# A graph network layer pair on one core: by-edge weights kept in PSUM, window sums and constants sharing two banks

## The chip, the cores and the metric

The kernel runs on one core of one Trainium2 chip. The metric is the device time of one execution in microseconds (us). A profile is one execution, recorded by the hardware; its span runs from the first to the last instruction of the program. Engines are named as in the profile: PE (TensorE, matmuls; PEld its weight loads), DVE (VectorE), ACT (ScalarE), POOL (GpSimd, which issues the gathers), SP (SyncE, which issues the plain DMAs).

## The reference

A graph has 6250 nodes of 128 features and 100000 edges, sorted by their destination. Two layers run one after the other, each with a residual sum and a layer norm over the features.

```python
# layer 0: mean of messages
m = relu(nfeat[src] @ W_ne[:128] + (efeat @ W_edge) @ W_ne[128:] + b_ne)
neigh = segment_sum(m, dst) / max(count(dst), 1)
x = layernorm(x + neigh + x @ W_self + b_self)

# layer 1: attention over the edges (and a loop on each node), 4 heads of 32
xl = x @ w_l + b_l;  xr = x @ w_r + b_r
e = leaky_relu(xl[src] + xr[dst], 0.2)
logits = einsum('ehc,hc->eh', e, att)
ex = exp(logits - segment_max(logits, dst)[dst])
alpha = ex / segment_sum(ex, dst)[dst]
out = segment_sum(xl[src] * alpha, dst) + bias
out = (out - out.mean()) / (out.std() + 1e-5) * ln_w + ln_b
x = layernorm(x + out)
```

## The kernel before

The edges are cut into 196 groups of 512 (four tiles of 128). Because they are sorted, the destinations of a group lie in a window of 96 node rows. The function `near` holds both edge stages. Each stage gathers the source rows of its groups from DRAM by indirect DMAs on POOL (`gather`, L339, four to a group, 128 rows each).

**First edge stage** (`e0`, steps of the loop at L559). Messages are formed on PE, DVE and ACT, and the sums over a window are matmuls with a one-hot matrix (`onehot`, L393 to L397: 1 where the edge's destination is that row of the window). The change touches only where `onehot` finds its constant row 0 to 95, `iota_q`.

**Second edge stage** (`e1`, L593 to L912). The order on each engine is the order in which the lines of the step loop (L887) are written; nothing is rescheduled. Step `s` does, in this order:

- `gather1(s + 4)`: the four gathers on POOL. A group's rows stay in one of 30 buffers until `values` has read them.
- `store_sums` and the planned `out_load`, `m_load`, `m_logits`.
- `copy_both(s - 1)` on ACT, `both(s)` on PE: `z` becomes xl[src] + xr[dst], transposed, in PSUM (`pz`).
- `leaky(s - 1)` on DVE, `logits(s - 2)` on PE, `onehot_t(s + 1)` on ACT.
- for each group due in this step: `sums(u)` (four matmuls into `pa`, then `old` on DVE takes the window of the group before, scaled, and one more small matmul adds its last row), `keep_sums(u)` (ACT copies `pa` to SBUF).
- for each group due in the next step: `values_w(u)` (ACT copies weight and maximum by edge into `v`), `values(u)` (DVE multiplies the gathered rows by the weights), `onehot(u)`.
- the rest of the plan: steps of the softmax chain, and outputs of finished blocks (`out_weights`, `output` with `ready`, which multiplies by ln_w).

**The softmax chain.** Twelve groups (nine and seven in the last two) make a macro; its logits lie in one tile with a row for each head and group. `M_STEPS` lists ten functions, one to a step, that find the running maxima by scans, the maximum carried over from one group to the next, and the weights: `m_logits`, `m_forward`, `m_back`, `m_ends`, `m_groups`, `m_before`, `m_maxima`, `m_weights`, `m_left`, `m_ready`. The last three turn weights and maxima from rows to edges: transposes into the PSUM tile `pw` (`by_edge`), and ACT copies of it into the SBUF tile `wm` (`keep_by_edge`). A macro's first group is due `len(M_STEPS) + 1` steps after the chain begins; from 30 steps before the last group on, two groups may fall due in one step. `output` of a block comes five steps after its last group is stored.

**PSUM.** There are eight banks. Before, the second stage has two for `pz`, two for `plg` (logits), two for `pa`, one for `pw` (also used by `m_ends` and `m_before`), and one, `rows_q`, for constants that DVE alone reads: `iota_q` and `lnw_q` (ln_w). `rows_q` lives through both stages.

Of the kernel before, what the change touches and what calls it, by code (L numbers as in the profile page):

```python
# [9 lines left out]
F32 = mybir.dt.float32  # L10
F32R = mybir.dt.float32r
# [6 lines left out]
P = 128  # L18
N = 6250
E = 100000  # L20
D = 128
# [53 lines left out]
def gnn_resnorm(  # L75
# [268 lines left out]
    def near():  # L344
        ctx = ExitStack()
        with ctx:
# [13 lines left out]
            kps = ctx.enter_context(tc.tile_pool(name="nearp", bufs=1, space=PSUM))  # L360
            rows_q = kps.tile([P, W + D], F32, name="rows_q")
            iota_q, lnw_q = rows_q[:, 0:W], rows_q[:, W:]
            nc.vector.tensor_copy(iota_q, iota_w)
            nc.vector.tensor_copy(lnw_q, lnw_b)
# [28 lines left out]
            def onehot(pool, g, dtype):  # L393

                a = pool.tile([P, G, W], dtype, name="a")
                nc.vector.tensor_tensor(a, over(iota_q, G), spread(dl[:, g * G:(g + 1) * G], W), op=OP.is_equal)  # L396
                return a  # L397
# [13 lines left out]
            with tc.tile_pool(name="e0", bufs=3) as pool, tc.tile_pool(name="e0p", bufs=2, space=PSUM) as ps, \  # L411
# [7 lines left out]
                pt = ps1.tile([P, 2, G // 2, P], F32, name="pt")  # L419
                EF, XG, FT, PX, XS, PH, OH, PA, WIN = {}, {}, {}, {}, {}, {}, {}, {}, {}  # L420
# [138 lines left out]
                for s in range(-2, max(steps) + 1):  # L559
# [22 lines left out]
                    if group(2) is not None:  # L582
                        OH[s - 2] = onehot(pool, s - 2, F32R)
# [9 lines left out]
            with tc.tile_pool(name="e1", bufs=3) as pool, tc.tile_pool(name="e1m", bufs=2) as mp, \  # L593
# [104 lines left out]
                def m_ends(m):  # L698
                    m.pe = ps1.tile([P, S], F32, name="pw")
                    for i in range(2):  # L700
                        nc.tensor.transpose(m.pe[0:1, i * P:i * P + m.R], m.ends[:, i:i + 1], ident[0:m.R, 0:m.R])

                def m_groups(m):
# [4 lines left out]
                    for i in range(2):  # L708
                        nc.vector.tensor_copy(seq[:, i, :, 1:],
                                              m.pe[0:1, i * P:i * P + m.R].rearrange("p (h g) -> p h g", h=H))  # L710
# [9 lines left out]
                def m_before(m):  # L720
                    m.pv = ps1.tile([P, S], F32, name="pw")
                    nc.tensor.matmul(m.pv[0:m.R, 0:1], m.prev_r.rearrange("p h g -> p (h g)"), ones[0:1, 0:1],
                                     start=True, stop=True)

                def m_maxima(m):
                    R = m.R
                    prev = mp.tile([R, 1], F32, name="prev")
                    nc.vector.tensor_copy(prev, m.pv[0:R, 0:1])
# [13 lines left out]
                def by_edge(m, i, t):  # L742
                    m.pw = ps1.tile([P, S], F32, name="pw")
                    for j in range(G):
                        nc.tensor.transpose(m.pw[:, j * m.R:(j + 1) * m.R], t[:, j * P:(j + 1) * P],
                                            ident[0:m.R, 0:m.R])

                def keep_by_edge(m, i):
                    nc.scalar.copy(m.wm[:, :, i].rearrange("p j h g -> p j (h g)"),
                                   m.pw[:, 0:G * m.R].rearrange("p (j r) -> p j r", j=G))  # L750

                def m_weights(m):
                    R = m.R
                    m.wm = mp.tile([P, G, 2, H, m.mg], F32, name="wm")
# [5 lines left out]
                    nc.tensor.matmul(m.pw[:, G * R:(G + 1) * R], ones[0:R, :], dg, start=True, stop=True)  # L760
# [12 lines left out]

# [113 lines left out]
                for s in range(stop + 1):  # L887
# [20 lines left out]
                    for u in due.get(s + 1, ()):  # L908
                        values_w(u)
                        values(u)  # L910
                        OH[u] = onehot(pool, u, F32)
# [333 lines left out]
```

## Time and profile before

The median of three runs is 2222.46 us (2222.4 to 2223.11). The profiled execution took 2217.53 us, with a span of 2215.8 us and a mean granted PE clock of 0.837.

The span falls into these stretches. Each number is busy time in us; PEclk is the granted clock as a share of full speed.

| stretch, us | length | PE | DVE | ACT | POOL | PEclk |
|---|---|---|---|---|---|---|
| 45 to 1016: first edge stage | 971 | 633.0 | 589.6 | 207.1 | 734.8 | 0.78 |
| 1016 to 1052: between the stages | 36 | 14.5 | 26.0 | 3.3 | 0.1 | 0.59 |
| 1052 to 1190: second stage, no group due yet | 138 | 101.6 | 27.7 | 54.2 | 105.1 | 0.72 |
| 1190 to 1880: one group a step | 690 | 580.3 | 396.8 | 321.5 | 526.3 | 0.99 |
| 1880 to 2057: also two groups or none | 177 | 154.8 | 127.2 | 82.1 | 135.5 | 0.89 |
| 2057 to 2156: after the last gather | 99 | 70.8 | 74.3 | 18.8 | 0.0 | 0.64 |
| 2156 to 2216: last outputs and norm | 60 | 1.1 | 43.1 | 23.1 | 0.0 | 0.50 |

A row of the timeline gives start and length in us, the engine, the line, the operation, and what it writes and reads; in square brackets stands the idle time before it and what ended it. POOL counts as busy while an indirect DMA is being prepared; between two of them there are 0.30 us in which it waits for nothing that the profile shows. In the groups, `xN` is the number of instructions, then busy us and mean ns of one, then the idle time before them.

### The profile page before, as it was taken

The numbers are of one execution on the slowest core, as the hardware profiler recorded it, in microseconds if no ns is written. First come the engines' busy times: TensorE is split into PE (matmuls) and PEld (weight loads), VectorE is DVE, ScalarE is ACT, GpSimd is POOL, SyncE is SP. The second block draws the span as 40 slices with busy tenths as digits, with TensorE's granted clock in tenths as the row PEclk, the third lists the DMA queues.
The fourth block names the chain that finished last, engine by engine and source line by source line (L and its number), as shares of the span: only waits on it lengthen the run. The fifth ranks groups of instructions, "written<-read, shape, count | busy, mean of one in ns | idle before, by whom it ended". The sixth has DMA issues, their size and how long they took to land.

```text
span 2215.8 us, 26713 instructions
## 1 busy us (share of the span) xinstructions
PE 1569.5 (71%) x6565; PEld 878.3 (40%) x6565; DVE 1304.2 (59%) x3709; ACT 713.4 (32%) x1723; POOL 1511.0 (68%) x1575
## 2 busy tenths in 40 slices
PE   3786566566556566665678888888888888889760
PEld 2664444444344444443123333333333333434440
DVE  5664455556556666777123555555565666677777
ACT  1331211121112222221344444444444444444214
POOL 3777777777777777772777777777777777777100
PEclk9997767777777778776778999999999999989755
DMA  4654344434444444432433444444444444443102
GB/s 122 155 116 90 88 95 95 98 89 103 100 102 96 103 105 108 106 89 59 134 103 101 114 112 113 114 115 112 116 116 113 113 111 113 116 119 100 29 23 62
DMA packets 292630, 225.34 MB, mean 102 GB/s; under 512 B 143289, under 2 KB 247591, under 8 KB 292466
## 3 DMA queue, kind: packets, MB, share of 16 engines
q1 hardware_dynamic: 240624, 120.21, 20.5%
q0 software_dynamic: 50048, 102.60, 19.6%
q8 instruction: 56, 0.92, 0.2%
q10 hardware_dynamic: 1794, 0.73, 0.2%
q14 instruction: 108, 0.88, 0.1%
HBM read 189.85 MB, written 33.52 MB: 101 GB/s over the span
## 4 chain that ended last, share of the span: by engine, by line
DMA 21%; POOL 21%; PE 19%; DVE 19%; issue 17%; ACT 2%; DVEq 0%; SPq 0%; ACTq 0%; POOLq 0%
POOL xg L339 21%; DMA xg<-xw_t,src_i 11%; DMA xg<-xl_t,src_i 9%; PE pa L790 5%; PE plg L661 3%; PE pz L635 3%; DVE a L396 3%; DVE msg L480 2%; PE pz L633 2%; PE pa L796 2%; DVE v L781 1%; PE ph L462 1%; DVE win L494 1%; DVE ln_st L211 1%; DVE old L794 1%
## 5 line engine op out<-in xcount | busy, mean ns | idle before, releaser
L339 POOL DMA_INDIRECT xg<-xl_t,src_i x782 | 767.0, 981 | 274.4 <-issue 173.2
L339 POOL DMA_INDIRECT xg<-xw_t,src_i x738 | 697.3, 945 | 224.9 <-issue 186.5
L642 DVE SCALAR_TENSOR_TENSOR z<-z,pz 128x512 f32<-128x512 f32 x196 | 134.6, 686 | 381.0 <-ACT z L639 375.3
L471 DVE TENSOR_TENSOR ph<-ph,xg 128x512 f32<-128x512 f32 x185 | 129.5, 700 | 336.1 <-DMA xg<-xw_t,src_i 302.3
L476 ACT ACTIVATE msg<-ph 128x512 fp32r<-128x512 f32 x196 | 117.3, 599 | 549.1 <-DVE ph L471 513.8
L633 PE MATMUL pz<-ident,xg 128*128 128x128 f32 x784 | 189.3, 317 | 148.0 <-DMA xg<-xl_t,src_i 131.7
L462 PE MATMUL ph<-wc,fT 128*128 128x256 f32 x784 | 286.5, 502 | 0.0
L489 PE MATMUL pa<-win,sel 96*1 96x129 f32 x390 | 90.2, 321 | 248.8 <-DVE win L494 247.5
L790 PEld LDWEIGHTS pa<-v,a 128*96 128x96 f32 x1568 | 200.9, 175 | 157.7 <-issue 111.8
L790 PE MATMUL pa<-v,a 128*96 128x136 f32 x1568 | 248.2, 305 | 8.6 <-DVE a L396 5.2
L661 PE MATMUL plg<-z,attw 128*48 128x512 f32 (+2 forms) x392 | 229.1, 669 | 0.0
L635 PE MATMUL pz<-ds,xr 96*128 96x512 f32 x392 | 219.4, 643 | 0.0
L396 DVE TENSOR_TENSOR a<-rows_q,dl 128x384 fp32r<-128x384 f32 (+1 forms) x392 | 214.7, 548 | 0.0
L801 ACT COPY win<-pa 96x136 f32<-96x136 f32 x196 | 52.5, 268 | 480.9 <-PE pa L796 448.9
L462 PEld LDWEIGHTS ph<-wc,fT 128*128 128x128 f32 x784 | 182.2, 251 | 59.1 <-issue 31.4
L633 PEld LDWEIGHTS pz<-ident,xg 128*128 128x128 f32 x784 | 95.6, 145 | 263.8 <-DMA xg<-xl_t,src_i 186.8
L487 PE MATMUL pa<-msg,a 128*96 128x258 f32 x784 | 180.5, 364 | 0.0
L626 ACT ACTIVATE ds<-ds,nb 96x512 f32<-96x512 f32 x196 | 142.1, 725 | 8.7 <-DMA xr<-xr_t 8.6
L627 ACT ACTIVATE ds<-ds,ones 96x512 f32<-96x512 f32 x196 | 141.5, 722 | 6.4
L480 DVE SCALAR_TENSOR_TENSOR msg<-ph,msg 128x512 fp32r<-128x512 f32 x196 | 135.6, 692 | 3.4 <-ACT msg L476 3.4
L487 PEld LDWEIGHTS pa<-msg,a 128*96 128x96 f32 x784 | 134.6, 212 | 1.0 <-PE pa L487 0.4
L639 ACT COPY z<-pz 128x512 f32<-128x512 f32 x196 | 113.5, 579 | 66.5 <-PE pz L635 66.4
(204 smaller groups left out, 1776.1 us busy)
## 6 DMA issues: line engine op xcount, KB each, us to landing
ds<-dpad SPq DMA_DIRECT2D x196, 192.0 KB
ef<-in_edge_attr_dram SPq DMA_DIRECT2D x48, 512.0 KB
xg<-xl_t,src_i POOLq DMA_INDIRECT x782
xg<-xw_t,src_i POOLq DMA_INDIRECT x738
out_t<-win SPq DMA_DIRECT2D x196, 51.0 KB
sum_t<-win SPq DMA_DIRECT2D x196, 48.4 KB
xr<-xr_t SPq DMA_DIRECT2D x196, 48.0 KB
s<-out_t SPq DMA_DIRECT2D x47, 68.0 KB
```

Source lines behind the costliest of these rows:

```text
L339: nc.gpsimd.indirect_dma_start(out=to, out_offset=None, in_=table[0:min(table.shape[0], NP), :], in_offset=bass.IndirectOffsetOnAxis(ap=in ...
L396: nc.vector.tensor_tensor(a, over(iota_q, G), spread(dl[:, g * G:(g + 1) * G], W), op=OP.is_equal)
L462: nc.tensor.matmul(ph[:, 2 * i:2 * i + 2, :], fT[:, i, :], wc, start=i == 0 or g >= RAW, stop=g >= RAW, skip_group_check=g < RAW)
L480: nc.vector.scalar_tensor_tensor(msg[:, :, 1, 0:D], PH.pop(g), 0.0, msg[:, :, 0, 0:D].bitcast(F32), op0=OP.max, op1=OP.subtract)
L487: nc.tensor.matmul(pa, a[:, j, :], msgs[g % 3][:, j], start=j == 0, stop=j == G - 1)
L626: nc.scalar.activation(DS[g], DS[g], AF.Abs, bias=nb[0:W, g:g + 1])
L627: nc.scalar.activation(DS[g], DS[g], AF.Relu, bias=ones[0:W, 0:1], scale=-1.0)
L633: nc.tensor.matmul(pz[:, j * P:(j + 1) * P], XG[g][:, j, :], ident, is_transpose=True, start=j == 0, stop=False, skip_group_check=True)
L635: nc.tensor.matmul(pz, XR.pop(g), DS.pop(g), start=False, stop=True, skip_group_check=True)
L642: nc.vector.scalar_tensor_tensor(Z[g], Z[g], SLOPE, PZ.pop(g), op0=OP.mult, op1=OP.max)
L661: nc.tensor.matmul(m.plg, attw[m.mg][:, m.mg - i:m.mg - i + m.R], Z.pop(g), start=i == 0, stop=i == m.mg - 1)
L790: nc.tensor.matmul(pa, a[:, j, :], v[:, j].rearrange("p h c -> p (h c)"), start=j == 0, stop=j == G - 1)
```

## The change

Four things are done in the second edge stage, and one in the first:

1. The tiles `pw` and `wm` become one PSUM tile of a full bank, in two buffers: the transposes write weights and maxima by edge straight to the layout that `values_w` and `values` read, and these read PSUM. `keep_by_edge` and the step `m_ready` go; the chain has nine steps, so a macro's groups are due one step earlier.
2. The window sums `pa` no longer come from a pool of two: even groups use the bank `pb[0]`, odd ones `pb[1]`.
3. The constants `iota_q` and `lnw_q` stand beside the sums in `pb[0]`. The bank `rows_q` goes.
4. The small results of `m_ends` and `m_before` stand beside the sums in `pb[1]` (`few`), not in `pw`.
5. The first stage gets an `iota_q` of its own, handed to `onehot`.

```diff
-            kps = ctx.enter_context(tc.tile_pool(name="nearp", bufs=1, space=PSUM))
-            rows_q = kps.tile([P, W + D], F32, name="rows_q")
-            iota_q, lnw_q = rows_q[:, 0:W], rows_q[:, W:]
-            nc.vector.tensor_copy(iota_q, iota_w)
-            nc.vector.tensor_copy(lnw_q, lnw_b)
...
-            def onehot(pool, g, dtype):
+            def onehot(pool, g, dtype, iota_q):
...
+                iota_q = ps1.tile([P, W], F32, name="iota_q")
+                nc.vector.tensor_copy(iota_q, iota_w)
...
+                pb = [ps1.tile([P, 4 * P], F32, name=f"pb{i}") for i in range(2)]
+                HS = H * HV
+                iota_q, lnw_q, few = pb[0][:, HS:HS + W], pb[0][:, HS + W:HS + W + D], pb[1][:, HS:HS + 2 * P]
+                nc.vector.tensor_copy(iota_q, iota_w)
+                nc.vector.tensor_copy(lnw_q, lnw_b)
...
                 def m_ends(m):
-                    m.pe = ps1.tile([P, S], F32, name="pw")
                     for i in range(2):
-                        nc.tensor.transpose(m.pe[0:1, i * P:i * P + m.R], m.ends[:, i:i + 1], ident[0:m.R, 0:m.R])
+                        nc.tensor.transpose(few[0:1, i * P:i * P + m.R], m.ends[:, i:i + 1], ident[0:m.R, 0:m.R])
...
                 def m_before(m):
-                    m.pv = ps1.tile([P, S], F32, name="pw")
-                    nc.tensor.matmul(m.pv[0:m.R, 0:1], m.prev_r.rearrange("p h g -> p (h g)"), ones[0:1, 0:1],
+                    nc.tensor.matmul(few[0:m.R, 0:1], m.prev_r.rearrange("p h g -> p (h g)"), ones[0:1, 0:1],
                                      start=True, stop=True)
...
                 def by_edge(m, i, t):
-                    m.pw = ps1.tile([P, S], F32, name="pw")
                     for j in range(G):
-                        nc.tensor.transpose(m.pw[:, j * m.R:(j + 1) * m.R], t[:, j * P:(j + 1) * P],
+                        nc.tensor.transpose(m.wm[:, j, i].rearrange("p h g -> p (h g)"), t[:, j * P:(j + 1) * P],
                                             ident[0:m.R, 0:m.R])
-
-                def keep_by_edge(m, i):
-                    nc.scalar.copy(m.wm[:, :, i].rearrange("p j h g -> p j (h g)"),
-                                   m.pw[:, 0:G * m.R].rearrange("p (j r) -> p j r", j=G))
...
                 def m_weights(m):
                     R = m.R
-                    m.wm = mp.tile([P, G, 2, H, m.mg], F32, name="wm")
+
+                    m.pw = ps.tile([P, 4 * P], F32, name="pw")
+                    m.wm = m.pw[:, 0:2 * G * R].rearrange("p (j k h g) -> p j k h g", j=G, k=2, h=H)
...
-                    nc.tensor.matmul(m.pw[:, G * R:(G + 1) * R], ones[0:R, :], dg, start=True, stop=True)
+                    nc.tensor.matmul(m.pw[:, 2 * G * R:(2 * G + 1) * R], ones[0:R, :], dg, start=True, stop=True)
...
                 def m_left(m):
-                    keep_by_edge(m, 0)
                     m.cb = mp.tile([P, H, m.mg], F32, name="cb")
-                    nc.vector.tensor_copy(m.cb, m.pw[:, G * m.R:(G + 1) * m.R].rearrange("p (h g) -> p h g", h=H))
+                    nc.vector.tensor_copy(m.cb, m.pw[:, 2 * G * m.R:(2 * G + 1) * m.R].rearrange("p (h g) -> p h g", h=H))
                     by_edge(m, 1, m.mx)
 
-                def m_ready(m):
-                    keep_by_edge(m, 1)
-
-                M_STEPS = (m_logits, m_forward, m_back, m_ends, m_groups, m_before, m_maxima, m_weights, m_left,
-                           m_ready)
+                M_STEPS = (m_logits, m_forward, m_back, m_ends, m_groups, m_before, m_maxima, m_weights, m_left)
...
-                    pa = PA[u] = ps.tile([W, H * HV], F32, name="pa")
+                    pa = PA[u] = pb[u % 2][0:W, 0:HS]
```

More of the change, by code (lines that the diff above doesn't have):

```diff
@@ L582, in near @@
                     if group(2) is not None:
-                        OH[s - 2] = onehot(pool, s - 2, F32R)
+                        OH[s - 2] = onehot(pool, s - 2, F32R, iota_q)
                     do(window, 4)
@@ L709, in m_groups @@
                         nc.vector.tensor_copy(seq[:, i, :, 1:],
-                                              m.pe[0:1, i * P:i * P + m.R].rearrange("p (h g) -> p h g", h=H))
+                                              few[0:1, i * P:i * P + m.R].rearrange("p (h g) -> p h g", h=H))
                     run = mp.tile([1, H, mg + 1], F32, name="run")
@@ L727, in m_maxima @@
                     prev = mp.tile([R, 1], F32, name="prev")
-                    nc.vector.tensor_copy(prev, m.pv[0:R, 0:1])
+                    nc.vector.tensor_copy(prev, few[0:R, 0:1])
                     fp = mp.tile([R, S], F32, name="fp", bufs=1)
@@ L910, in near @@
                         values(u)
-                        OH[u] = onehot(pool, u, F32)
+                        OH[u] = onehot(pool, u, F32, iota_q)
                     planned(s, but=FIRST)
```

## The prediction

> **What bounds the kernel now.** I read the page's busy table and costliest groups first, then the stretches of the second edge stage, the list of waits, and the timeline in three places: a steady step, a long gather, and the end of the stage.
>
> ```profile
> PE 1569.5 (71%) x6565; PEld 878.3 (40%) x6565; DVE 1304.2 (59%) x3709; ACT 713.4 (32%) x1723; POOL 1511.0 (68%) x1575
> L339 POOL DMA_INDIRECT xg<-xl_t,src_i x782 | 767.0, 981 | 274.4 <-issue 173.2
> L749 ACT COPY wm<-pw 128x192 f32<-128x192 f32 x30 | 9.3, 312 | 1.4 <-PE pw L760 0.9 <-PE pw L745 0.5
> ```
>
> The second edge stage issues 782 gathers on POOL from 1051.9 to 2057.0 us. A gather lasts 0.944 us at the median and the next starts 0.30 us later: 1.249 us, four to a group, 5.0 us a step. POOL never stands idle longer than that 0.3 us there (the largest "issue" wait in the list of waits is 0.3). The other engines wait for gathers: PE loses 131.7 us before pz L633. So up to about 1900 us the stage lasts as long as POOL issues, and what follows the last gather (2057.0 to 2154.9 us, the last group's sums) is a chain through DVE, PE and ACT.
>
> Some gathers are longer. In this row the gather begins 0.04 us after `values` and lasts 1.46 us:
>
> ```profile
> 1178.41 0.68 DVE L781 TENSOR_TENSOR v<-xg,wm 128x512 f32<-128x512 f32 x1
> ...
> 1178.45 1.46 POOL L339 DMA_INDIRECT xg<-xl_t,src_i  x1 [0.30 <-issue]
> ```
>
> I put all 782 gathers beside the DVE rows: where L781 runs 0.14 us after a gather's start, 59 are long, and their excess over 0.944 us sums to 15.7 us. All excess of all gathers is 28.9 us (scans, `pen`, `mx` and `old` make the rest).
>
> The end of the stage, one step with two groups (DVE, PE, ACT; each line is start, length, engine, line, tiles):
>
> ```profile
> 2135.55 0.29 DVE L794 TENSOR_TENSOR old<-pa,cb 96x136 f32<-96x136 f32 x1
> ...
> 2135.90 0.61 PE L796 MATMUL pa<-old,sel 96*1 96x136 f32 x2 [2.08 <-DVE old L794]
> ...
> 2136.44 2.13 PE L790 MATMUL pa<-v,a 128*96 128x136 f32 x8
> 2136.55 0.27 ACT L801 COPY win<-pa 96x136 f32<-96x136 f32 x1 [0.67 <-PE pa L796]
> ...
> 2136.85 0.30 DVE L794 TENSOR_TENSOR old<-pa,cb 96x136 f32<-96x136 f32 x1 [1.00 <-ACT win L801]
> 2137.06 0.68 DVE L781 TENSOR_TENSOR v<-xg,wm 128x512 f32<-128x512 f32 x1
> ...
> 2138.50 0.61 PE L796 MATMUL pa<-old,sel 96*1 96x136 f32 x2
> ...
> 2139.14 0.27 ACT L801 COPY win<-pa 96x136 f32<-96x136 f32 x1 [2.33 <-PE pa L796]
> ...
> 2139.31 0.40 ACT L777 COPY v<-wm 128x32 f32<-128x32 f32 x2
> ...
> 2142.19 0.29 DVE L794 TENSOR_TENSOR old<-pa,cb 96x136 f32<-96x136 f32 x1
> ```
>
> The reader is to see the order: `values` for the next groups (2137.06) starts while PE still multiplies this step's second group (2136.44 to 2139.11). It has no need of the ACT copy L777, which comes 2.25 us later. From `old` to the next `old` is 6.64 us.
>
> **The change, part by part.**
>
> *Removed: 34 copies L749 on ACT.* 34 x 0.31 = 10.6 us of an engine that is 32% busy: 0. They end one wait, though (below).
>
> *`values` reads its weights from PSUM.* Its length: L781 is 678 ns with both inputs in SBUF, L642 is 686 with one in PSUM, same size; +0.01 x 196 = 2 us of DVE, hidden under the gathers. With one SBUF input left, the 59 collisions go. The price lies between 0 (its new place in the step lets other rows fall on gathers) and -15.7; I take **-12**, by the rows: L642 and L396, which read PSUM and SBUF, run as often and go with 3 long gathers, 0.3 us. Here a rule speaks against this term. The Trainium skill ("SBUF — State Buffer", section "Who interferes with whom") has DVE instructions with two SBUF inputs contend with a GpSimd instruction that reads SBUF, but infers that descriptor generation needs only the write side, and so that tensor_tensor does not hold it up; by that inference the term would be 0 and the sum 12 us higher. The 1.46 us row shows the hold.
>
> *New waits.* Two engines' accesses to one bank are put in order in this kernel, reads too: `cb` L765 waits 41.4 us for the ACT copy L749 of the same bank in the trace. In the changed program, as built, `values` of each group waits for ACT's `values_w` of that group; every second `onehot` waits for PE's sums in the bank that holds the constants; the sums of an even group wait for DVE's last read of that bank, which is `ready`'s multiplication in a step with an output; `m_ends` and `m_before` wait for ACT's copy of the sums. `values_w` stands on ACT behind `keep_sums`, which waits for the step's last sums. So `values`, and behind it on DVE `onehot`, the planned work X of the step (outputs, scans) and the next step's `leaky` and `old`, start after PE's sums instead of beside them. PE waits for `old`, then POOL for nothing.
>
> Step with one group, full clock. PE alone: 0.59 + 0.86 + 0.97 + 1.10 + 0.37 = 3.9 us (the chain of waits at 2059 us: pz, pz, plg, pa, last sum). The new chain: win and v 0.5, `values` 0.60, `onehot` 0.47 (starts in the timeline), X, `leaky` 0.61, `old` and its wait 0.29, last sum 0.35: 2.8 + X. An output is X = 2.0, its first half 0.8, scans 1.1 to 1.5, `m_maxima` 2.1: at most some 5 us, against 5.0 to 5.07 for POOL. Before about 1880 us it is hidden by the gathers; without that cover each output would cost about 1 us, some 30 in all.
>
> Step with two groups beside gathers (18 steps, from about 1905 us). PE: 5.3 us (last sums 2059.34 to 2064.65). New chain: 1.8 (both sums) + 0.45 + 2.14 + X + 0.60 + 0.33 = 5.3 + X, so X comes on top. X by the plan written in the kernel, a number for each step that has any: 0.8 + 2.0 + 1.0 + 2.0 + 3.5 = 9.3 us in the first run of such steps, 1.1 + 1.1 + 1.5 = 3.7 in the second, 1.1 + 1.5 + 0.9 = 3.5 in the third. In the steps without groups that lie between, PE has under 3 us of work and half of the first 13.0 can be caught up; the last can't. 6.5 + 3.5 = **+10**; bounds 3.5 and 16.5. Six waits of `m_ends`/`m_before` for the ACT copy, 0.4 each: **+2**.
>
> Steps after the last gather, at half clock as above (7 passages from a step with two groups to the next). New: `old` to last sum 0.35, both sums to their end 3.21 (2135.90 to 2139.11), ACT 0.45, `values` and `onehot` twice 2.14, X 2.98: 9.13 against 6.64, **+2.5** each. Where the first of the pair is even (180 to 188) and the step has an output, its eight matmuls (2.06) wait for X as well instead of running under it: another 2.06 + 0.07 - 0.35 = 1.8. Three passages at 4.3 and four at 2.5: +23. One step fewer in the chain saves the wait for the last copy: 2130.43 + 0.25 less the end of the transposes at 2130.39, and some issue, 0.3 to 1: together **+22**. At full clock the pair ends in 1.81 and the eight in 1.10: 3 x 1.9 + 4 x 1.1 = 10, the lower bound; the upper is 30, as some waits of `m_weights` on DVE (1.2 each) fall there too.
>
> *Constants.* One copy more (L363 0.26, L364 0.28 us), and they now stand at the start of the stages, where POOL waits 36.3 us for stores: 0; uncovered 0.8. `few` takes the place of pw's bank: no cost but the two waits counted. First stage: same instructions.
>
> Sum: -12 + 10 + 2 + 22 = **+22 us**. The profiled execution has a span of 2215.8 and a time of 2217.53; the median of the runs is 2222.46, 4.9 above it. 2222.5 + 22 = **2244**.
>
> The Trainium skill ("PSUM — Partial Sum Buffer", the section on bank collisions) wants PSUM guarded by bank and quadrant and not by address, reads against reads included, and names different banks as the remedy; this change goes the other way. If only addresses counted, the +34 would fall away and -12 stay.
>
> **The rivals.**
> 1. *The stage leaves POOL before 1880 us.* For: 2.8 + X is near 5 us wherever an output falls, the matmul waits on even groups add 0.3, and the granted clock dips to 0.86 to 0.91 in some 12 us stretches after 1800. Against: single steps without X need 3.9 and catch up. If half of the 30 us shows and the gather gain is lost under it: 2244 + 15 = 2259, or up to 2272.
> 2. *The gathers win.* DVE's work is bunched behind the sums, so all 28.9 us of excess go, and the clock stays full behind the last gather: -28.9 + 4 + 2 + 10 = -13, 2210: faster. It decides where the gathers end earlier by more than the 17 us that the rest then costs. For: POOL bounds 1000 us, the end only 100. Against: scans and `pen` keep two SBUF inputs, and PE's clock fell to 0.5 from 2084 us on, after a shorter wait than the new ones.
> 3. *Both cancel*: 12 to 16 of gain against the 16 of the lower bounds: 2222.
> 4. *It doesn't do what it says*: the waits are in the built program, so that isn't left.
>
> **How the numbers follow.** Forecast 2244 (own range 2228 to 2256) 0.55; rival 1 0.20; rival 2 0.16; rival 3 0.09. A measurement of this kernel tells 0.2%, 4.4 us, from no change (the three runs lie within 0.7). Slower 0.76, with a little of rival 3 lost to either side; same 0.08; faster 0.16. The range leaves out the far parts of rivals 1 and 2: 2216 to 2264.
>
> **What would show it.** Gathers behind `values` back at 0.944 us and the last gather near 2045; `values` directly behind `values_w` in every step; DVE idle before it, released by ACT; PE's sums released by `ready` L336 in steps with an even group; from the last gather to the last sums some 34 us longer (22 later, from a gather 12 earlier). It is wrong if the gathers end as before, if the passages at the end stay at 6.6 us, or if POOL waits for buffers before 1880.

## The result, and the profile after

The changed kernel takes 2291.17 us (median of four runs, 2278.91 to 2296.3), against 2222.43 us for the kernel before in the same measurement: a ratio of 1.0306 (95% interval 1.0279 to 1.0334). The forecast was 2244 with a range up to 2264: the direction is right, the size is not. The profiled execution has a span of 2294.6 us (before 2215.8) and took 2296.3 us; the mean granted PE clock fell from 0.837 to 0.806.

Seven of the experiments' runs (e1 to e4, and e9 to e11) come from two measurements in which the kernel before took 2820 us: the gathers paused there, in the first stage too (in e3, 61 pauses beyond the usual 0.30 us, 222 us in all; none in the profile before). Why is not known. The chip's number does not tell: e9 to e11 stand on record under that of e5 to e8, where the kernel before took 2219.6 us. From those seven runs only rows that do not hang on the gathers are read, and their kernels, or a close form, were run again in another measurement ("elsewhere" below).

From the page of the changed kernel, its busy table and groups (what it writes and reads, count, busy us, mean ns, idle before and what ended it):

```profile
PE 1604.7 (70%) x6565; PEld 905.8 (39%) x6565; DVE 1307.4 (57%) x3710; ACT 699.5 (30%) x1689; POOL 1501.4 (65%) x1575
...
L339 POOL DMA_INDIRECT xg<-xl_t,src_i x782 | 757.1, 968 | 330.1 <-issue 219.0
...
L775 DVE TENSOR_TENSOR v<-xg,pw 128x512 f32<-128x512 f32 x196 | 134.4, 686 | 355.1 <-ACT v L771 355.1
```

The same 6565 matmuls keep PE busy 35 us longer than before (1569.5). The gathers are 9.9 us shorter in sum, but POOL stands idle 56 us more. And `values` (L775) was released 169 times by the ACT copy `values_w` (L771), after 355 us of idle DVE. Before, DVE was not idle in front of it:

```profile
L781 DVE TENSOR_TENSOR v<-xg,wm 128x512 f32<-128x512 f32 x196 | 132.9, 678 | 0.0
```

In the list of waits (engine, line and releaser: us in total, times, longest) three of PE's waits for DVE have grown, for `old`, `cb` (14.6 us before) and `dg` (3.6 us before). Before:

```profile
PE pa L796 <- DVE old L794: 20.6, 13, 3.1
```

After, with a fourth that is new, the sums of an even group behind `ready` (L336):

```profile
PE pb L790 <- DVE old L788: 66.4, 50, 3.3
...
PE pb L784 <- DVE xl L336: 23.9, 10, 4.4
...
PE pw L746 <- DVE cb L763: 21.2, 14, 1.8
PE pw L759 <- DVE dg L755: 21.2, 14, 3.5
```

The list puts three more waits of this fourth kind, 19.9 us in all, on L811, the instruction behind `ready`: PE starts 0.15 us after L336 ends in each of them.

Where the time went is read by groups. I took the start of the ACT copy of the window sums (L795; L801 before) of each group, counted from the stage's first gather, and subtracted the same of the kernel before:

| up to the sums of group | what runs there | lag in us | gained or lost since the row above |
|---|---|---|---|
| 0 | first sums, a chain of nine steps instead of ten | -6.8 | -6.8 |
| 140 | one group a step | +31.8 | +38.6 |
| 175 | two groups or none a step, gathers still running | +52.3 | +20.5 |
| 195 | mostly behind the last gather | +76.1 | +23.8 |

With 1.9 us before the stage and 0.8 behind it this is the 78.8 us between the spans. Half of the loss lies where one group falls due in a step. One trace is one execution: in that of e16, the same kernel again, the three rows are +28.6, +20.5 and +23.9 us, so the first of them varies by 10 us. The stretches of the changed kernel (length; busy us of PE, PEld, DVE, ACT, POOL with counts; granted PE clock; DMA share; GB/s):

```profile
1190.00:1530.00 340.00, 292.86 (x1250) 137.27 (x1250) 178.04 (x432) 149.38 (x348) 258.31 (x269) 0.92 0.42 112
1530.00:1880.00 350.00, 290.31 (x1207) 139.69 (x1205) 201.75 (x583) 146.32 (x346) 256.99 (x266) 0.88 0.40 109
```

Before, the clock was 1.00 and 0.99 in these two stretches, with 1281 and 1292 matmuls instead of 1250 and 1207. PE is as busy as it was, but at a lower clock. From the first sums to those of group 120, 2301 matmuls each: 518.4 us of busy PE in 614.5 us before, 546.0 in 643.9 after. PE's matmuls last 27.6 us longer, and 29.4 us are lost. That the two are near each other does not yet show that one is the other; the experiments below price the clock.

One macro shows how that comes. Its timeline (start, length, engine, line, operation; idle before and its end in brackets), from the sums of one step to the matmul after `cb`:

```profile
1606.60 1.17 PE L784 MATMUL pb<-v,a 128*96 128x136 f32 x8
1607.08 0.68 DVE L737 TENSOR_TENSOR lg<-lg,mx 48x512 f32<-48x512 f32 x1
...
1609.02 0.69 DVE L646 SCALAR_TENSOR_TENSOR z<-z,pz 128x512 f32<-128x512 f32 x1 [1.13 <-ACT z L643]
1609.63 0.29 DVE L788 TENSOR_TENSOR old<-pb,cb 96x136 f32<-96x136 f32 x1
...
1609.97 0.39 PE L790 MATMUL pb<-old,sel 96*1 96x136 f32 x2 [2.20 <-DVE old L788]
...
1610.57 0.19 ACT L771 COPY v<-pw 128x32 f32<-128x32 f32 x1
1610.79 0.69 DVE L775 TENSOR_TENSOR v<-xg,pw 128x512 f32<-128x512 f32 x1 [0.87 <-ACT v L771]
1611.39 0.55 DVE L391 TENSOR_TENSOR a<-pb,dl 128x384 f32<-128x384 f32 x1
1611.86 0.23 DVE L755 TENSOR_SCALAR dg<-ident,sc 48x48 f32<-48x48 f32 x1
...
1612.15 0.66 PE L759 MATMUL pw<-dg,ones 48*128 48x48 f32 x2 [1.41 <-DVE dg L755]
...
1613.64 1.91 PE L639 MATMUL pz<-ds,xr 96*128 96x512 f32 x2
...
1615.48 1.94 PE L665 MATMUL plg<-z,attw 128*48 128x512 f32 x2
...
1621.23 0.45 PE L746 MATMUL pw<-ident,mx 48*128 48x48 f32 x4 [1.75 <-DVE cb L763]
```

DVE starts `values` only behind the ACT copy, which stands behind the sums. So `maxima` (L733 to L739) pushes `leaky` (L646) and `old` back. `leaky` waits another 1.13 us for ACT's copy of `z`, which stands behind the exponentials of `maxima` on ACT. So PE waits 2.20 us for `old`; then `dg` waits on DVE behind `values` and the one-hot, and PE waits 1.41 us in the weights step; then `cb` in the left step, 1.75 us. After the first two waits pz L639 and plg L665 take 1.91 and 1.94 us instead of 1.02 and 1.06. The granted clock of these stretches shows why (start and end; length; busy us of PE with count; granted clock; DMA share; GB/s):

```profile
1611.86:1618.69 6.83, 6.54 (x16) 0.50 0.37 90
...
1622.10:1625.52 3.42, 3.42 (x6) 0.50 0.44 125
```

In the 3.41 us ahead of each, PE was busy 0.77 and 1.66 us at a clock of 1.00.

Steps in which nothing else is planned take 3.9 us, as forecast; the weights and left steps take 8.7 and 7.4 us, and gathers for a step take 5.0. Three of twelve steps are of this long kind, and the others catch up only a part. Up to group 42 the lag still falls back to -5.7 us; from there it grows. (By the plan no output stands beside the first 36 groups, and three or four in twelve from group 96 on.) From 1693.7 us on POOL itself waits for buffers that `values` frees late (17 times; in e16 from 1809 us on).

### The profile page after: what moved, and what is told of

The parts are those of the page before. It is cut to its first block, busy times and chain, and to the rows that moved or that the text cites. A ratio compares the mean times of both kernels' runs of the same rounds, so it can differ in the third digit from the quotient of the medians.

```text
span 2294.6 us, 26567 instructions
## 1 busy us (share of the span) xinstructions
PE 1604.7 (70%) x6565; PEld 905.8 (39%) x6565; DVE 1307.4 (57%) x3710; ACT 699.5 (30%) x1689; POOL 1501.4 (65%) x1575
## 3 DMA queue, kind: packets, MB, share of 16 engines
q1 hardware_dynamic: 240624, 120.21, 19.6%
## 5 line engine op out<-in xcount | busy, mean ns | idle before, releaser
L339 POOL DMA_INDIRECT xg<-xl_t,src_i x782 | 757.1, 968 | 330.1 <-issue 219.0
L775 DVE TENSOR_TENSOR v<-xg,pw 128x512 f32<-128x512 f32 x196 | 134.4, 686 | 355.1 <-ACT v L771 355.1
L784 PEld LDWEIGHTS pb<-v,a 128*96 128x96 f32 x1568 | 211.5, 182 | 226.1 <-issue 152.9
L784 PE MATMUL pb<-v,a 128*96 128x136 f32 x1568 | 258.5, 314 | 58.0 <-DVE xl L336 23.9
L665 PE MATMUL plg<-z,attw 128*48 128x512 f32 (+2 forms) x392 | 246.3, 715 | 0.0
L639 PE MATMUL pz<-ds,xr 96*128 96x512 f32 x392 | 240.3, 699 | 0.0
L646 DVE SCALAR_TENSOR_TENSOR z<-z,pz 128x512 f32<-128x512 f32 x196 | 132.9, 678 | 137.2 <-ACT z L643 124.3
L637 PE MATMUL pz<-ident,xg 128*128 128x128 f32 x784 | 163.3, 322 | 55.7 <-DMA xg<-xl_t,src_i 44.0
L795 ACT COPY win<-pb 96x136 f32<-96x136 f32 x196 | 52.5, 268 | 455.3 <-PE pb L790 441.8
```

The costliest lines, as they stand in the source:

```text
L339: nc.gpsimd.indirect_dma_start(out=to, out_offset=None, in_=table[0:min(table.shape[0], NP), :], in_offset=bass.IndirectOffsetOnAxis(ap=in ...
L637: nc.tensor.matmul(pz[:, j * P:(j + 1) * P], XG[g][:, j, :], ident, is_transpose=True, start=j == 0, stop=False, skip_group_check=True)
L639: nc.tensor.matmul(pz, XR.pop(g), DS.pop(g), start=False, stop=True, skip_group_check=True)
L646: nc.vector.scalar_tensor_tensor(Z[g], Z[g], SLOPE, PZ.pop(g), op0=OP.mult, op1=OP.max)
L665: nc.tensor.matmul(m.plg, attw[m.mg][:, m.mg - i:m.mg - i + m.R], Z.pop(g), start=i == 0, stop=i == m.mg - 1)
L775: nc.vector.tensor_tensor(V[u][:, :, :, 2:], XG.pop(u).rearrange("p j (h c) -> p j h c", h=H), m.wm[:, :, 0, :, u - m.g0].unsqueeze(3).to_ ...
```

## The experiments

Mean length of a step, from one group's copy of the sums to the next, by the planned work behind it (groups 0 to 139, steps with no output; 17 or 24 steps in the first column, 7 in each of the others; us):

| kernel | nothing planned | maxima | weights | left |
|---|---|---|---|---|
| before | 5.11 | 5.06 | 5.11 | 5.26 |
| changed | 3.94 | 6.15 | 8.74 | 7.44 |
| e5, weights copied to SBUF | 4.90 | 5.77 | 5.34 | 5.37 |
| e6, sums in banks of their own | 3.86 | 6.16 | 8.49 | 7.90 |
| e7, values first | 4.84 | 5.04 | 4.72 | 4.84 |
| e8, dg and cb first | 4.31 | 6.57 | 6.35 | 4.23 |
| e12, ACT copy first | 4.77 | 5.79 | 5.91 | 5.37 |
| e16, changed kernel again | 3.97 | 6.27 | 8.37 | 6.98 |
| e17, PE's waits filled | 4.13 | 6.64 | 7.01 | 6.10 |

**Which half of the change (e1 and e5; e2 and e6).** Two kernels that each undo one half. In the first, the weights come from SBUF:

```diff
                     by_edge(m, 1, m.mx)
+                    m.ws = mp.tile([P, G, 2, H, m.mg], F32, name="ws")
+                    nc.scalar.copy(m.ws.rearrange("p j k h g -> p (j k h g)"), m.pw[:, 0:2 * G * m.R])
...
-                    nc.scalar.copy(V[u][:, :, :, 0:2], m.wm[:, :, :, :, u - m.g0].rearrange("p j k h -> p j h k"))
+                    nc.scalar.copy(V[u][:, :, :, 0:2], m.ws[:, :, :, :, u - m.g0].rearrange("p j k h -> p j h k"))
...
-                                            m.wm[:, :, 0, :, u - m.g0].unsqueeze(3).to_broadcast([P, G, H, C]),
+                                            m.ws[:, :, 0, :, u - m.g0].unsqueeze(3).to_broadcast([P, G, H, C]),
```

> The changed kernel, but one ACT copy per macro (128x384) puts weights and maxima into SBUF, and values and values_w read them there; the fixed banks, the constants in them and the nine steps stay. Theory A (the loss comes from values, which waits for ACT's values_w of the same PSUM bank and so for PE's sums, and delays dg and cb behind it): values runs beside the sums again, the weights and left steps fall from 8.7 and 7.4 us to 5 or less, the last gather ends near 2060 us instead of 2104, the time is 2225 to 2245 (the end keeps the waits of the shared sum banks). Theory B (the shared banks of sums and constants cause it: one-hot behind PE's sums, even sums behind the output): little changes, 2270 to 2295.

> The kernel of weights_sbuf once more (weights and maxima copied to SBUF once per macro; fixed banks, constants in them and nine steps stay), since in the runs before the gathers themselves paused on that chip, in the first stage too, and the kernel before took 2821 us. Where the kernel before takes about 2222 us: theory A (values waits for ACT's values_w and so for PE's sums, and delays dg and cb) 2225 to 2245; theory B (shared banks of sums and constants) 2270 to 2295.

In the second, the sums leave the shared banks, and `few` becomes a part of `m.pw`, which is taken from its pool in `m_ends`:

```diff
-                    pa = PA[u] = pb[u % 2][0:W, 0:HS]
+                    pa = PA[u] = ps.tile([W, H * HV], F32, name="pa")
...
-                    ready(pool, b0, n, lnw_q)
+                    ready(pool, b0, n)
...
-                        OH[u] = onehot(pool, u, F32, iota_q)
+                        OH[u] = onehot(pool, u, F32, iota_w)
```

> The changed kernel, but the sums have their own two banks as before, the constants are read from SBUF, and m_ends and m_before use the macro's weight bank; weights and maxima stay in PSUM and the chain has nine steps. Theory A (values behind values_w behind the sums): still slow, 2265 to 2295, weights step over 7 us; some of the end (even sums behind the output, 5 to 10 us) comes back. Theory B (shared sum banks): 2225 to 2245. With one-hot and the last multiplication reading two SBUF inputs, some gathers beside them get long again (up to 15 us over all gathers, which costs nothing while POOL waits for buffers).

> The kernel of own_banks once more (sums in their own banks, constants from SBUF, weights and maxima in PSUM, nine steps). Where the kernel before takes about 2222 us: theory A 2265 to 2295 with the weights steps over 7 us; theory B 2225 to 2245.

With the paused gathers: 1.0117 (1.0077 to 1.0156) and 1.0109 (1.004 to 1.0179) times the kernel before, which separates nothing. Elsewhere: weights in SBUF 2243.57 us, ratio 1.0113 (1.0096 to 1.0131); own banks 2273.86 us, 1.0245 (1.0227 to 1.0264). So theory A holds: the weights in PSUM carry most of it. (The weights and left steps of e5, 5.3 and 5.4 us, are a little above the 5 expected.) The shared banks carry a part that lies at the end: from group 175 to 195 the changed kernel loses 23.8 us, with own banks 14.5.

The first kernel's page shows something else (gathers, and `values` with both inputs in SBUF again):

```profile
L339 POOL DMA_INDIRECT xg<-xl_t,src_i x782 | 782.1, 1000 | 274.8 <-issue 183.8
...
L777 DVE TENSOR_TENSOR v<-xg,ws 128x512 f32<-128x512 f32 x196 | 132.8, 678 | 0.5 <-ACT f L820 0.3
```

`values` waits 0.5 us in all instead of 355, and the gathers are 25 us longer than in the changed kernel: 80 of them start beside `values` (which runs 0.06 us after the gather's start) and carry 23.8 us of excess over 0.944 us. The last gather ends at 2072.6 us. All gathers together take 15.1 us longer than before, of 20.1 us by which the span is longer, so they are most of what this kernel is still behind.

**Order alone (e3 and e7).** The place in the step, and a fourth buffer for the two tiles that are now made earlier:

```diff
-                a = pool.tile([P, G, W], dtype, name="a")
+                a = pool.tile([P, G, W], dtype, name="a", bufs=4)
...
-                    V[u] = pool.tile([P, G, H, HV], F32, name="v")
+                    V[u] = pool.tile([P, G, H, HV], F32, name="v", bufs=4)
...
                     planned(s, only=FIRST)
+                    for u in due.get(s + 1, ()):
+                        values_w(u)
+                        values(u)
+                        OH[u] = onehot(pool, u, F32, iota_q)
...
-                    for u in due.get(s + 1, ()):
-                        values_w(u)
-                        values(u)
-                        OH[u] = onehot(pool, u, F32, iota_q)
                     planned(s, but=FIRST)
```

> The changed kernel with only the order altered: values_w, values and onehot of the next step's groups are issued at the start of the step, ahead of copy_both, leaky and the sums (four buffers for v and the one-hot instead of three). Every wait for a bank stays in the program, but values_w no longer stands behind keep_sums. Theory A: DVE works while PE transposes, weights and left steps under 5.5 us, the gathers set the time again without the collisions: last gather near 2040 us, time 2195 to 2230. Theory C (the two PE waits for dg and cb in the weights and left steps are there whatever stands before them on DVE): these steps stay over 7 us, time 2265 or more.

> The kernel of values_first once more (values_w, values and one-hot at the start of the step; all else as in the changed kernel). Where the kernel before takes about 2222 us: theory A 2195 to 2230, last gather near 2040; theory C (PE's waits for dg and cb are there whatever stands before them on DVE) 2265 or more.

With the paused gathers 1.0022 (0.9986 to 1.0058). Elsewhere 2230.82 us, 1.006 (1.0041 to 1.008): 0.8 us above the range of theory A. The last gather ends at 2046.6 us, 10.4 before that of the kernel before, and the weights and left steps are under 5 us: theory C falls. What I had not reckoned with is the end, 117 us from the last gather to the last sums against 98. There two `values` and two one-hots now stand ahead of `leaky`; that this is the reason no run shows by itself.

**dg and cb first (e4 and e8).** `values` stays late; only the two small operations PE waits for, and the masked `mx`, move ahead of it, to the start of the weights step (`m_scale`) and of the left step (`m_cb`):

```diff
+                def m_scale(m):
+                    nc.vector.tensor_scalar(m.dg, ident[0:R, 0:R], m.sc, None, op0=OP.mult)
+                    nc.vector.scalar_tensor_tensor(m.mx, m.pen[:, 1:], -1.0, m.mx, op0=OP.is_lt, op1=OP.mult)
...
+                def m_cb(m):
+                    m.cb = mp.tile([P, H, m.mg], F32, name="cb")
...
-                FIRST = (m_load, out_load, m_logits)
+                FIRST = (m_load, out_load, m_logits, m_scale, m_cb)
```

> The changed kernel with only dg, the masked mx and cb issued on DVE at the start of the weights and left steps instead of behind values and onehot. Theory H (PE's waits of 1.4 to 1.75 us for dg and cb, and the half clock that follows each, are most of the loss before 1880 us): the two steps fall from 8.7 and 7.4 to 4.5 to 5 us, the lag at group 175 falls from 54 us to under 15, time 2240 to 2255. Rival (every step with planned work loses, and the clock has nothing to do with it): only the waits themselves go, 17 x 3.1 = 53 us at most and about half of it under the gathers, lag at 175 over 30 us, time 2265 to 2285.

> The kernel of scale_first once more (dg, masked mx and cb at the start of the weights and left steps). Where the kernel before takes about 2222 us: theory H (PE's waits for dg and cb and the half clock behind each are most of the loss before 1880) 2240 to 2255, the two steps 4.5 to 5 us each, lag at group 175 under 15 us; rival 2265 to 2285, lag over 30 us.

With the paused gathers 1.0075 (1.004 to 1.011). Elsewhere 2257.9 us, 1.0177 (1.016 to 1.0194): 3 us above the range of theory H, with the lag at group 175 as it said, 12.4 us instead of 52.3. The left step falls to 4.23 us; the weights step, 6.35, misses the 4.5 to 5 that were expected. The rest, 23.9 us from there to group 195, is that of the changed kernel.

**The ACT copy alone (e9 and e12).** The narrowest edit, with a fourth buffer for `v`:

```diff
-                    V[u] = pool.tile([P, G, H, HV], F32, name="v")
+                    V[u] = pool.tile([P, G, H, HV], F32, name="v", bufs=4)
...
                     planned(s, only=FIRST)
+                    for u in due.get(s + 1, ()):
+                        values_w(u)
...
                     for u in due.get(s + 1, ()):
-                        values_w(u)
                         values(u)
```

> The changed kernel with one thing moved: the ACT copy values_w (0.19 us) is issued at the start of the step, ahead of copy_both and keep_sums (four buffers for v); values, one-hot and the planned work keep their places on DVE behind old. Theory A in its narrow form (all that values lost is the wait for an ACT copy queued behind the sums): weights and left steps under 5.5 us, clock back to 0.98, last gather 2045 plus or minus 5, from there to the last sums about 100 us as before: time 2205 to 2225. Rival (DVE is simply too late with values and one-hot in front of dg and cb): those steps stay at 6 to 7 us and the time at 2235 to 2260.

> The kernel of copy_first once more (only the ACT copy values_w is moved to the start of the step), since in the runs before the gathers paused by themselves and the kernel before took 2820 us. Where the kernel before takes about 2222 us: theory A in its narrow form 2205 to 2225, weights and left steps under 5.5 us, last gather 2045 plus or minus 5; rival (DVE too late with values and one-hot in front of dg and cb) 2235 to 2260.

With the paused gathers 1.0119 (1.0082 to 1.0157). Elsewhere 2218.81 us, 0.9985 (0.9972 to 0.9999), as theory A said; the last gather ends at 2049.6 us and POOL never waits for a buffer. So the loss goes with the place of one 0.19 us copy. The fourth buffer is not what gains: in the changed kernel ACT's only waits before L771 are for `values` (26 times, 19.6 us) and for one transpose (0.5 us), never for the sums L784 that free a buffer of `v`. The weights step, 5.9 us, is a little above the 5.5 expected, and the clock is 0.95 from the first sums to group 120. Behind the last gather the shared bank still shows (timeline; the multiplication by ln_w, and PE's eight matmuls of an even group):

```profile
2099.96 0.25 DVE L336 TENSOR_TENSOR xl<-xl,pb 128x128 f32<-128x128 f32 x1
...
2100.26 2.13 PE L784 MATMUL pb<-v,a 128*96 128x136 f32 x8 [2.63 <-DVE xl L336]
```

**What the shared bank still costs (e13), and dg and cb on top (e10 and e14).** In e13 `ready(pool, b0, n, lnw_q)` becomes `ready(pool, b0, n)`, which reads ln_w from SBUF; e10 is e9, and e14 is e13, with the edit of e4.

> As copy_first, and the last multiplication of an output reads ln_w from SBUF, so that the sums of an even group no longer wait for it in their bank. Theory (the shared bank costs the end some 8 us by that wait, as between own_banks and the changed kernel: 9.3 us from group 175 to 195): 4 to 8 us below copy_first, 2200 to 2218, all of it behind group 175. Rival (the shared bank costs by one-hot, which waits for even sums): within 2 us of copy_first.

> As copy_first, and dg, the masked mx and cb at the start of the weights and left steps too. If copy_first already takes PE's waits for dg and cb under the gathers, this adds nothing before 2045 us and at most 5 us behind the last gather: within 5 us of copy_first. If dg and cb are late by themselves, 15 to 30 us below copy_first.

> As copy_first_lnw, and dg, the masked mx and cb at the start of the weights and left steps. Behind the last gather one macro's weights and left steps fall: 0 to 5 us below copy_first_lnw, nothing before. If dg at the start delays leaky and the output behind it as much, no gain.

e13: 2212.4 us, 0.9967 (0.9949 to 0.9985), 6.4 us below e12 and, of its lead of 7.0 in the traces at group 195, 5.9 behind group 175. e10, with the paused gathers: 1.0192 (1.0149 to 1.0235), 24.3 us above e9 instead of within 5. While the gathers pause I do not read the one against the other; e14 repeats the question elsewhere. e14: 2214.23 us, 0.9967 (0.9957 to 0.9977): no gain over e13. So e13, the change with the copy at the step's start and ln_w in SBUF, beats both kernels, the one before by 0.3%.

**Does PE's standing still lower its clock (e11, e15, e16, e17)?** These add work. PE multiplies the identity into unused columns of the weight bank where it stood still, ahead of the matmul with `dg` and ahead of `cb`:

```diff
+                def fill(m, n):
+                    for i in range(n):
+                        nc.tensor.matmul(m.pw[:, (2 * G + 1) * m.R:(2 * G + 1) * m.R + 80], ident, ident[:, 0:80],
+                                         start=True, stop=True)
...
                     by_edge(m, 0, m.lg)
+                    fill(m, 6)
...
                 def m_left(m):
+                    fill(m, 6)
```

In e11 there are eight at each place, in e15 six. e17 adds nine more in `sums`, ahead of `old`, in the step behind `m_maxima`, and fills only macros that start before group 132; for that the bank `m.pw` is taken from its pool one step earlier, in `m_maxima`.

> The changed kernel with work added, nothing moved: eight matmuls (128x128 by 80 columns, into unused columns of the weight bank) on PE ahead of the dg matmul in the weights step and eight ahead of cb in the left step, where PE stands still for 1.4 and 1.75 us now. Clock theory (it is PE's standing still that halves the granted clock for the following 5 us): pz and plg behind the waits return from 1.9 to about 1.05 us, the weights step falls from 8.7 to 6 to 7 us and the left step from 7.4 to 5.5 to 6.5, time 2250 to 2280 although PE does more. Rival (the clock falls for another reason, or the pauses are only waits): pz and plg stay at 1.9, time 2290 to 2310.

> The changed kernel with six added matmuls (128x128 by 80 columns, 0.25 us each at full clock) ahead of the dg matmul and six ahead of cb. Clock theory: pz and plg of the step behind go from 2.1 to 1.2 us each in most macros (they did behind the left step with eight such matmuls), lag at group 175 falls from 52 us to 25 to 40, time 2260 to 2285 although PE does 51 us more work. Rival (the pauses matter only as waits): the steps keep their 8.7 and 7.4 us or more, time 2290 to 2310.

> The changed kernel itself, beside the filled one on the same chip: 2285 to 2300 where the kernel before takes about 2222; weights and left steps 8.7 and 7.4 us.

> The changed kernel with all three places filled where PE stands still in a macro, in the eleven macros that start before group 132 only (so that the end is as in the changed kernel): nine matmuls (128x128 by 80 columns, 0.25 us each at full clock) ahead of the wait for old in the step behind m_maxima, six ahead of dg, six ahead of cb; 21 x 0.25 = 5.3 us of added work for each macro. Six fills in two places left the weights step at half clock, because the 2.2 us wait for old ahead of it was not filled. Clock theory: pz and plg behind the weights step return to 1.2 us too, the weights step goes from 8.7 to 6 to 6.5 and the left step to 6.1, group 140 comes 15 to 30 us earlier than in the changed kernel, time 10 to 30 us lower although PE does 58 us more work. Rival (standing still is not what lowers the clock): pz and plg behind the weights step stay at 2.1 us, and the time is 0 to 20 us higher.

e11, with the paused gathers, 1.0253 (1.0216 to 1.0291); e15 2304.29 us, 1.0378 (1.0354 to 1.0402). The times missed the clock theory's ranges. The rows did not wholly: behind the left step pz and plg (two matmuls each, summed) went from mostly 2.1 to 1.19 and 1.22 us in all of the first eleven macros of e15, behind the weights step they stayed at 2.1 in nine of them. The 2.2 us wait for `old` ahead of that step was not filled there, which e17 tests. And at the end, where no gather hides anything, e15 pays for the fills (8.6 us more lag at group 195 than the changed kernel, 0.7 less at 175).

With all three places filled, e17 takes 2273.83 us, 1.0246 (1.0213 to 1.0279); the changed kernel in the same measurement (e16) 2285.47, 1.029 (1.0258 to 1.0323). Eleven times 21 matmuls more (56.5 us of busy PE), and 11.6 us less; group 140 comes 14.8 us earlier, just short of the 15 expected. Only 5.9 us of that stand at group 120, up to which macros are filled. The other 8.9 come behind it, where nothing is filled; there POOL waits for buffers in e16 (from 1809 us on) and not yet in e17 (from 2002 us on), but no run shows that this is the reason. The PE timeline of e17:

```profile
1414.18 2.13 PE L765 MATMUL pw<-ident 128*128 128x80 f32 x18
...
1416.94 1.57 PE L765 MATMUL pw<-ident 128*128 128x80 f32 x12
...
1419.41 1.02 PE L639 MATMUL pz<-ds,xr 96*128 96x512 f32 x2
1420.36 1.06 PE L665 MATMUL plg<-z,attw 128*48 128x512 f32 x2
```

L765 is the fill. In the same order as in the changed kernel, with the same wait of DVE behind ACT, pz L639 and plg L665 are back at 1.02 and 1.06 us. So it is behind both steps in nine of the eleven filled macros; behind the weights step both are in none of the same eleven of the changed kernel and of e16. The weights step is 7.0 us (6 to 6.5 expected) and the left step 6.1, each with 1.5 us of added matmuls inside.

## Why the prediction was wrong, and where it was right

**The wait was named rightly.** `values` behind `values_w` behind PE's sums, 169 of 196 times; moving that one copy (e12) takes away the whole loss. That `few` costs the two waits of `m_ends` and `m_before` is right as well: 30 of them, 0.36 us each (0.4 forecast).

**The step that failed: "Before about 1880 us it is hidden by the gathers".** It forecast 0 and measured +38.6 us from group 0 to 140 (+28.6 in e16). The sum 2.8 + X is a chain through DVE in one step, and it was compared with 5.0 us step by step, as if each step stood alone and the clock were full. For a step with nothing planned it holds (3.9), and up to group 42 the gathers do hide the rest. Three things were missing.

First, ACT in the `maxima` step, which the sum put at nothing: 2.8 + 2.1 gives 4.9 us, 6.15 were measured, and `leaky` waits at least 1.13 us for ACT in each of these steps up to group 140. Second, `m_weights` and `m_left` are not only X on DVE: PE waits inside them, for `dg` and `cb`, which the new order puts behind `values` and the one-hot; I had those waits only as a vague 1.2 us at the end. With these two and the masked `mx` moved to the front, and `values` as late as in the changed kernel, next to nothing is lost up to group 140 (e8: lag -7.3 us at group 0, -6.8 at 140). The `maxima` step still takes 6.57 us there, so alone it is caught up. Third, the stops of 2.20, 1.41 and 1.75 us in a macro put PE at half clock for most of two steps.

How much of the loss is the clock's is not shown in full. Up to group 120 the matmuls last 27.6 us longer beside 29.4 us lost (16.0 beside 19.4 in e16), but in e12 they last 12.8 us longer and 0.5 us is lost, so a lower clock alone can hide under the gathers. The fills of e17 give back 15.2 of the 28.6 us that e16 loses from group 0 to 140, and 11.6 us of its time. The rest is not split between the waits and the clock.

**Rival 1 is what happened, mis-sized.** It had the stage leave POOL before 1880 us; POOL's first wait for a buffer is at 1693.7 (1809 in e16), which was one of the prediction's own signs of being wrong, and the last gather ends at 2104.0, not near 2045. It priced the loss at up to half of 30 us plus the gather gain, 2272 at most, from outputs alone. Counted against 5.0 us a step up to group 140, the 33 `maxima`, weights and left steps (12 of them with an output or its first half as well) take 88.6 us too long, all other steps with an output or its first half 18.9.

**Gathers, -12: right, but not where it counts.** None of the gathers beside `values` is long any more. In the kernels where the rest does not hold them up, the stage's gathers take 12.3 (e7), 8.8 (e12) and 9.3 us (e13) less. In the changed kernel the gain is lost under POOL's waits for buffers. The prediction's 59 gathers and 15.7 us come out with `values` running 0.06 us after a gather's start; with the 0.14 us it names there are 61 and 17.0, which changes nothing. That the scans would hold more gathers in their new place (12.9 us of excess instead of 4.2) I allowed for only in the bound.

**Two-group steps beside gathers, +12: too low.** +20.5 measured from group 140 to 175, in e16 as well; the upper bounds came to 18.5. The sum took X on top of a full-clock PE; the clock in 1880 to 2057 us was 0.85, but 0.89 before, and what the sum lacked is not shown. It hangs on the same wait: with the copy first (e12) these groups lose 3.8 us.

**Behind the last gather, +22: right, in part by luck.** 23.8 us from group 175 to 195; from the last gather to the last sums 31.0 us more (97.9 before, 128.9 after; 34 forecast). A passage from one `old` to the next was forecast at 9.13 us, and 10.9 where an even group waits for an output: measured 9.15 (group 189 to 191), and 10.27, 11.05 and 10.28 (180 to 182, 182 to 184, 184 to 186). That is right. But the sum subtracted 6.64 from each, and before the change the last three took 7.41, 6.64 and 7.96, so they gained 9.6 us and not 12.9; the other steps from group 175 on gained 14.2, where the sum had 10. The wait of PE's sums for L336 is the one named: 23.9 us in ten times, of which nine fall ahead of group 175, and behind it 4.4 us and the three times, 19.9 us, that the list puts on L811.

**Small terms.** `values` takes 686 ns instead of 678, as forecast. The first sums come 6.8 us earlier by the shorter chain, for which I had no term; under the gathers it is worth nothing.

## What to carry to other kernels

Where two engines share a bank, read off the whole queue of the engine that goes first: a copy of 0.19 us is as late as what it stands behind, and moving it to the step's start made the change worth 0.3% (with ln_w read from SBUF) instead of costing 3%. When a wait is "hidden", add up the steps that have work of their own over a whole round of the pipeline, with every engine in the chain, and ask on which of them PE, not only the late engine, will stop; and look at the clock that follows each stop. A time that misses while the rows behave, as in e15, asks for a finer experiment, not for a new theory.

## What the runs showed of the hardware

PE's clock falls behind stops that are short. In the rows above PE stood still for 2.20 and 1.41 us with 0.8 us of work between, and the granted clock was 0.50 from 1611.86 to 1618.69 us; the stop of 1.75 us at 1619.5 was followed by 0.50 from 1622.10 to 1625.52. In the 3.41 us ahead of each fall PE was busy 0.77 and 1.66 us. The Trainium skill ("TensorE: Matmul & The Clock Gate", section "Part 1: The HAM clock gate (the "warmup" mystery)") has the clock set by activity windows of about 3.4 us that run freely, and gives "no PE-idle gaps >~3.4µs" as the rule. The lengths here, one and two such windows, agree with it; the rule, taken alone, does not: here the clock was halved behind stops well below 3.4 us, and filling them restored it behind both steps in nine of eleven macros. It does not fall each time: behind the left step of the changed kernel pz and plg stayed at full speed in two of the first eleven.

A gather that starts beside a DVE operation with two inputs in SBUF takes longer: 80 of 96 gathers and 23.8 us in e5 beside `values`, 84 of 101 and 14.7 us in e6 beside the one-hot that reads its row from SBUF. With one input in PSUM, as in the changed kernel, it is none of 88 beside `values` and one of 67, by under 0.05 us, beside the one-hot. In the prediction this row stood against the inference of "SBUF — State Buffer" (section "Who interferes with whom") that such an instruction does not hold descriptor generation; the experiments bear out the row.
